# Scan branches that make the step sizes first, a third step-size tile loaded one unit sooner, and two images whose last projection reads its inputs from on-chip memory

## The chip, the cores and the metric

The kernel runs on one core of a Trainium2 chip. The metric is device time in microseconds (us) of the whole program, which works through a batch of eight images in one launch. The engines are called by the names of the profile: PE (TensorE, matrix products), DVE (VectorE), ACT (ScalarE), POOL (GpSimd) and SP (SyncE, which here does nothing but issue DMAs). Each engine takes its instructions in one fixed order, and an instruction that waits holds up everything behind it on its engine. That holds for SP too: a DMA that waits for its source, or for its target to come free, delays all DMAs that stand behind it.

## The reference

Four layers, each `x = x + layer(group_norm(x))`, on x of shape (8, 256, 32, 32) in float32. Layer 0 is an attention with eight heads of 64 whose q and k are normalised over the positions; layers 1 and 2 are 3x3 convolutions. Layer 3 is the long one; cut to what matters here, with N = 1024 positions and 256 channels in four groups of 64:

```python
def mamba(xs, inw, convw, convb, xpw, dtw, dtb, alog, dp, outw):   # one of 4 branches
    u, z = jnp.split(xs @ inw.T, 2, axis=-1)                       # 128 channels each
    u = silu(causal_conv4(u, convw) + convb)
    xdbc = u @ xpw.T
    dt = softplus(xdbc[..., :DTR] @ dtw.T + dtb)                   # step sizes
    Bm, Cm = xdbc[..., DTR:DTR + DS], xdbc[..., DTR + DS:]         # DS = 16 states
    # h[t] = exp(dt[t] * A) * h[t-1] + (dt[t] * u[t]) * Bm[t];  y[t] = sum_s h[t] * Cm[t]
    y = selective_scan(u, dt, Bm, Cm, -jnp.exp(alog), dp)          # ... + u * dp
    return y * silu(z) @ outw.T

xn = layernorm(xs); xm = mamba of the 4 groups + skip * xn; gates and 1-D convolutions -> xm2
x_local  = depthwise conv3 of xm2
x_global = mha(xm2)                                                # 8 heads of 32
x_out = concat([x_local, x_global]) @ fc_w.T + fc_b                # "the last projection" of the title
x_out = gelu(layernorm(x_out)); 2-D depthwise conv, layernorm, proj_w
```

## The kernel before

Per image there are three groups of work. The *front* is attention layer 0 and the two 3x3 convolutions (`front_attention`, `front_convs`). The *scans* are the four branches of the selective scan (`scan_layers`). The *back* is everything after them (`back_layers` with the second attention, `back_out` with the product by `fc_w`, `back_end`). The front and the back are dense and live on PE; the scans live on ACT, DVE and POOL. The outer loop runs over images b = 0..7, and in iteration b `interleave` mixes the dense stream (back of image b-1, front of image b+1) with the scans of image b: after every so many units of dense cost, one step of the scans is written out (`PACE`, 1.8 units for the first image, 2.78 for the middle six, 1.6 for the last). In iteration 0 there is no back, in iteration 7 no front, and after iteration 7 the back of image 7 runs alone. A scheduler then lays out each engine's order: by priority (the order in which the code writes the instructions), and by when it reckons that data and buffers are there. `Paced` keeps a scan instruction from standing ahead of the dense instructions that the code wrote before it on the same engine, so what the scheduler believes about a load's arrival decides how many dense instructions come between two scan instructions.

*One branch.* `branch_front` makes a branch's inputs in six steps, separated by `yield`: 0 the product into `raw`; 1 the convolution and silu into `u`; 2 `low`, the product that gives B and C, stored to DRAM as `bc` and read back broadcast; 3 the product for the step sizes into `a`, and the exponential for softplus; 4 the rest of softplus into `dt`, which `store` writes to DRAM (two DMAs `dt_m<-dt`); 5 `du = dt * u`, stored likewise (`du_m<-a`). `fronts` decides when the steps of branches 1 to 3 are done: in units of the scan, counted so that unit 0 of branch i has its first loads at 16 i, step 0 falls at 16 i - 17, and steps 1 to 5 at 16 i - 12, -10, -8, -6 and -3.

*The scan units.* `scan_steps` cuts a branch into 16 units: two halves of the positions (h), four groups of states (q), two pairs of channel groups (gp). One unit covers 128 partitions x 2 x 512. Its stages: `load` (three units ahead; du at the start of a half, B and C for every second unit), `load_dt` (one unit ahead, the dt tile at the start of a half, four DMAs of 128 KB), `drive` on POOL (two ahead, du * B into an `hs` tile, L974), `decays` on ACT (two exponentials `da<-dt,a_neg` into a PSUM tile), `scan` on DVE (two `hs<-da,hs`, or `hs<-da,carry,hs` in the second half), `weigh` on POOL (hs * C, L1006), and `add_up` on PE (`y<-hs,sel`), which at the end of a half lets DVE do `u<-u,half_d,y`. dt tiles come from pool `dtp` with two buffers, one for each gp; a new half's tile therefore takes the place of the tile that the old half used.

*Two small pools.* `wsp` holds weight chunks of 128 x 512 (six buffers); their loads are issued from ACT and wait there until the chunk's buffer is free. `hp` holds 128 x 512 tiles (two buffers) into which ACT copies the result of an attention pair, `both` or `rs`, which SP then stores to DRAM.

*The inputs of the last projection.* At the end of `back_layers` the four tiles (two `local`, two `o`) are written to a DRAM tensor `mix` (four DMAs of 512 KB, L1312), and `back_out` reads them back (L1379) into four new tiles before `project_both("fcw", ...)` multiplies them: 32 matrix instructions `big<-mix,w`. The attention tiles `o` are divided by their sums at the very end, by way of a small exchange over DRAM (`few<-sums`, `inv<-few_inv`, `rs<-inv`, then DVE `o<-o,rs`).

Of the kernel before, what the change touches and what calls it, by code (L numbers as in the profile page):

```python
# [19 lines left out]
P = 128  # L20
C = 256
N = 1024
# [11 lines left out]
def preact_stack(ctx: ExitStack, tc: tile.TileContext, I, out, cols):  # L34
# [7 lines left out]
    wp = ctx.enter_context(tc.tile_pool(name="wp", bufs=1))  # L42
    sp = ctx.enter_context(tc.tile_pool(name="sp", bufs=2))

    wsp = ctx.enter_context(tc.tile_pool(name="wsp", bufs=6))
    xp = ctx.enter_context(tc.tile_pool(name="xp", bufs=1))
    vp = ctx.enter_context(tc.tile_pool(name="vp", bufs=1))
    tp = ctx.enter_context(tc.tile_pool(name="tp", bufs=12))
    hp = ctx.enter_context(tc.tile_pool(name="hp", bufs=2))
    ps_big = ctx.enter_context(tc.tile_pool(name="ps_big", bufs=2, space=PSUM))  # L50
    ps_acc = ctx.enter_context(tc.tile_pool(name="ps_acc", bufs=1, space=PSUM))

# [11 lines left out]
    def work(name):  # L64
        return tp.tile([P, TP], F32, tag="t", name=name)
# [10 lines left out]
    def mwork(name):  # L76
        return mp.tile([P, N], F32, tag="m", name=name)
# [4 lines left out]
    def da_tile():  # L82
        return ps_da.tile([P, HALF], F32, tag="da", name="da")
# [730 lines left out]
    def store(br, name, src):  # L814

        br[name] = dp.tile([32, 2, 4, HALF], F32, tag=name, name=name + "_m")
        for h in range(2):
            nc.sync.dma_start(
                out=br[name][:, h].rearrange("d g n -> g d n"), in_=src[:, HALVES[h]]
            )  # L820

    def branch_front(i, xn, br):


        j, rows = i // 2, slice((i % 2) * 64, (i % 2) * 64 + 64)
        for h in range(2):
            ps = da_tile()
            tensor.matmul(
                ps,
                minw[rows, j, 0:P],  # L830
                inner(xn[j])[rows, HALVES[h]],
                start=True,
                stop=True,
            )
            scalar.copy(raw[:, 3 + h * HALF : 3 + (h + 1) * HALF], ps)
        yield
        u = mp.tile([P, N], F32, tag="u", name="u", bufs=2)
        uu = u[:, 0:N]
        scalar.activation(
            uu,  # L840
            raw[:, 3 : 3 + N],
            AF.Identity,
            bias=col("convb", i),
            scale=col("convw", 4 * i + 3),
        )
        for k in range(3):
            vector.scalar_tensor_tensor(
                uu, raw[:, k : k + N], col("convw", 4 * i + k), uu, ALU.mult, ALU.add
            )
        th = raw[:, 3 : 3 + N]  # L850
        scalar.activation(th, uu, AF.Tanh, scale=0.5)
        vector.scalar_tensor_tensor(uu, th, 1.0, uu, ALU.add, ALU.mult)
        br["u"] = u
        yield

        low = mwork("low")
        for h in range(2):
            ps = da_tile()
            tensor.matmul(
                ps[0 : 2 * DS], mxpw[:, i], u[:, HALVES[h]], start=True, stop=True  # L860
            )
            scalar.copy(low[0 : 2 * DS, HALVES[h]], ps[0 : 2 * DS])
        br["bc"] = dp.tile([DS, 2, 2, HALF], F32, tag="bc", name="bc")
        for k in range(2):
            nc.sync.dma_start(
                out=br["bc"][:, :, k],
                in_=low[k * DS : (k + 1) * DS].rearrange("s (h n) -> s h n", h=2),
            )
        yield

        a, dt = mwork("a"), mwork("dt")
        aa, ee, dd = a[:, 0:N], raw[:, 3 : 3 + N], dt[:, 0:N]
        for h in range(2):
            ps = da_tile()
            tensor.matmul(
                ps, mdtw[:, i], u[:, HALVES[h]], start=True, stop=True
            )
            vector.tensor_scalar_add(a[:, HALVES[h]], ps, col("dtb", i))  # L880
        scalar.activation(ee, aa, AF.Abs)
        scalar.activation(ee, ee, AF.Exp, scale=-1.0)
        yield
        vector.tensor_scalar_add(dd, ee, 1.0)
        vector.scalar_tensor_tensor(ee, dd, -1.0, ee, ALU.add, ALU.subtract)
        scalar.activation(dd, dd, AF.Ln)
        vector.tensor_sub(dd, dd, ee)
        vector.scalar_tensor_tensor(dd, aa, 0.0, dd, ALU.max, ALU.add)
        store(br, "dt", dd)
        yield  # L890
        vector.tensor_mul(aa, dd, uu)
        store(br, "du", aa)
        yield

    def branch_back(i, xn, br):
# [27 lines left out]
    def scan_steps(branches):  # L923
# [14 lines left out]
        def load_groups(u, name):  # L938
            br, g = branches[u["i"]], u["gp"] * 2
            if u["q"] == 0:  # L940
                t = dtp.tile([P, 2, HALF], F32, tag=name, name=name)
                src = br[name][:, u["h"], g : g + 2].rearrange("d g n -> d (g n)")
                for s in range(4):
                    nc.sync.dma_start(
                        out=t[s * 32 : s * 32 + 32].rearrange("d g n -> d (g n)"),
                        in_=src,
                    )
                br[name, u["gp"]] = t
            u[name] = br[name, u["gp"]]
# [80 lines left out]
        for n in range(-3, len(units) + 2):  # L1030
            done = None
            for ahead, stage in (
                (3, load), (1, load_dt), (0, decays), (0, None),
                (0, scan), (-1, weigh), (2, drive),
            ):
                if stage is None:
                    yield
                elif 0 <= n + ahead < len(units):
                    stage(units[n + ahead])
            if n % 2 and 0 <= n - 3 < len(units) - 1:  # L1040
                done = add_up(units[n - 3 : n - 1])
            yield done

    def scan_layers(img):


        xt = img.pop("x")
        img["stats"] = group_stats(img.pop("mv"), da_tile)
        xn = [xm_tile("xn0"), xm_tile("xn1")]
        for t in xn:  # L1050
            zero_ends(t)
        group_norm(tiles(xt), img["stats"], [inner(t) for t in xn])
        img["xd"] = xdp.tile([P, 2, N], F32, tag="xd", name="xd")
        nc.sync.dma_start(out=img["xd"], in_=xt)
        sq = [mwork("ln_sq"), mwork("ln_sq")]
        yield
        yield from layer_norm(
            [inner(t) for t in xn], sq, BY_HALF, da_tile, affine("norm_w", "norm_b")
        )
        yield  # L1060
        branches = [{} for _ in range(NB)]
        for _ in branch_front(0, xn, branches[0]):
            yield

        def fronts():
            for i in range(1, NB):
                for n, _ in enumerate(branch_front(i, xn, branches[i])):
                    yield 16 * i - 12 + 9 * n // 4

        front, ending, due, n = fronts(), iter(()), 0, 0  # L1070
        steps = scan_steps(branches)
        while True:
            next(ending, None)
            while due is not None and n >= due:
                due = next(front, None)
            if next(steps, END) is END:
                break
            yield
            done = next(steps)
            if done is not None:  # L1080
                ending = branch_back(done, xn, branches[done])
            n += 1
            yield
        yield from ending
        img["xm"] = xn
# [123 lines left out]
    def back_layers(img, exact=False):  # L1209
# [82 lines left out]
        yield from project("fpw", fd, evac_x2)  # L1292


        img["mix"] = xdp.tile([4, P, N], F32, tag="mix", name="mix")
        local = []

        def add_local():
# [9 lines left out]
                next(img["begin"])  # L1308
        while len(local) < 2:
            add_local()  # L1310
        for t, part in enumerate(local + img.pop("o3")):
            nc.sync.dma_start(out=img["mix"][t], in_=part[:, 0:N])  # L1312

    def merge_weights():

# [58 lines left out]

    def back_out(img):

        srcs = [work("mix")[:, 0:N] for _ in range(4)]
        for t in range(4):
            nc.sync.dma_start(out=srcs[t], in_=img["mix"][t])  # L1379
        yield 0  # L1380
        xo = img["xo"] = [work("xo")[:, 0:N] for _ in range(2)]

        def evac_fc(m, ps):
            scalar.activation(xo[m], ps, AF.Identity, bias=fc_b[:, m : m + 1])

        yield from project_both("fcw", srcs, evac_fc)
# [124 lines left out]
    PLACES = [1, 4, 4, 4, 4, 5, 6, 8, 9, 10, 11, 12, 13, 14, 15, 16]  # L1511
    PLACES += [18, 20, 22, 24, 26, 27, 28, 29]
    EARLY = 3
    PACE = [1.8] + [2.78] * (batch - 2) + [1.6]
    imgs = [{} for _ in range(batch)]
    drain(
        amid(front_attention(image_of(0), imgs[0]), merge_weights(), (8,)),
        front_convs(imgs[0]),
# [51 lines left out]
    again = nc.values_load(flag[0:1, 0:1], min_val=0, max_val=1)  # L1570
    with tc.If(again > 0):
        with tc.For_i(0, batch, 1) as i:
            img = {}
            src = x_in[bass.ds(i, 1)].rearrange("o (t p) n -> p (o t) n", p=P)
            dst = out[bass.ds(i, 1)].rearrange("o c n -> (o c) n")
            drain(front_attention(src, img, True), front_convs(img), scan_layers(img))
            drain(back_layers(img, True), back_out(img), back_end(img, dst))
# [109 lines left out]
```

## Time and profile before

| | us |
|---|---|
| median of 3 runs | 6550.79 (6543.21 to 6555.45) |
| the profiled execution | 6534.17 |
| its span | 6532.5 |
| PE busy | 5503.0 (84% of the span) |
| DVE / ACT / POOL busy | 4003.1 / 2701.2 / 2737.3 |
| iteration 0 (from the store of image 0's `xd` to that of image 1's) | 375.0 to 1028.6 |
| iterations 1 to 6, each | 776.5, 765.3, 769.6, 761.2, 761.2, 761.3 |
| iteration 7, until DVE's scans end | 5623.7 to 6209 |
| the back of image 7, after that | to 6532.5 |

How to read the profile. Most instructions pass through one helper (L105), so they are told apart by the tiles they write and read: `da<-dt,a_neg` is the decay, `hs<-du,bc` is the drive. A row of the groups has count, then busy us, mean ns of one, then the engine's idle time just before such instructions and what ended it. In the timeline a number in square brackets is idle time of the engine before the entry. `SPq` is SP issuing a DMA. "issue" in the chain of waits is time in which the engine waited for nothing that the profile can name.

### The profile page before, as it was taken

Reading aid. Unit: us, or ns where it says so; the run is one execution under the profiler, and the core shown is the slowest. Engines: PE = TensorE matmul, PEld = TensorE weight load, DVE = VectorE, ACT = ScalarE, POOL = GpSimd, SP = SyncE. Lnnn points to the kernel's source line nnn. Section 1 sums busy time; section 2 is a strip of 40 time slices with the busy share of each in tenths; the row PEclk is TensorE's granted clock in tenths of the full one; section 3 lists DMA queues with packets and bytes.
Section 4 is the critical chain, followed back from the end, with each engine's and each line's share of the span. In section 5 each row is a group of like instructions: output and inputs, shape, how many; then the busy total and the mean of one; then the engine's idle time right before and its main releaser. Section 6 shows DMA issues by size and latency. Waiting matters only on the chain.

```text
span 6532.5 us, 52259 instructions
## 1 busy us (share of the span) xinstructions
PE 5503.0 (84%) x17318; PEld 1846.7 (28%) x17318; DVE 4003.1 (61%) x4613; ACT 2701.2 (41%) x3241; POOL 2737.3 (42%) x1302
## 2 busy tenths in 40 slices
PE   8886688899888988989889898899889898876496
PEld 2331133223332233222332233322332223311222
DVE  5247845577556775567756776567855777555622
ACT  3223424644255532644236442555326442344242
POOL 0006653634435353543517345263435435276500
PEclk9997889999899989999899998999899998988697
DMA  1022232323233132321223222231323212233301
GB/s 44 26 62 76 78 89 76 88 74 88 69 91 98 39 93 77 101 85 57 81 82 99 75 75 80 83 103 44 91 77 101 87 57 82 77 82 88 97 26 43
DMA packets 224761, 495.99 MB, mean 76 GB/s; under 512 B 61016, under 2 KB 102616, under 8 KB 223456
## 3 DMA queue, kind: packets, MB, share of 16 engines
q1 hardware_dynamic: 168032, 419.12, 22.2%
q10 hardware_dynamic: 56448, 73.43, 3.9%
q8 instruction: 139, 2.28, 0.1%
q14 instruction: 142, 1.16, 0.1%
HBM read 411.09 MB, written 72.88 MB: 74 GB/s over the span
## 4 chain that ended last, share of the span: by engine, by line
PE 53%; DVE 24%; issue 6%; DMA 6%; ACT 6%; POOL 4%; SPq 1%; ACTq 0%; DVEq 0%; POOLq 0%
PE big L105 33%; PE acc L105 11%; DVE hs L105 6%; PE da L105 5%; DVE p L105 4%; DVE dw L105 3%; POOL hs L1006 3%; PE y L105 3%; DVE u L105 2%; DVE t L105 1%; DMA du_m<-a 1%; POOL hs L974 1%; ACT p L105 1%; ACT da L105 1%; DMA dt<-dt_m 1%
## 5 line engine op out<-in xcount | busy, mean ns | idle before, releaser
L974 POOL TENSOR_TENSOR hs<-du,bc 128x1024 f32<-128x1024 f32 x512 | 1339.7, 2636 | 1623.2 <-DMA du<-du_m 683.0
L1006 POOL TENSOR_TENSOR hs<-hs,bc 128x1024 f32<-128x1024 f32 x512 | 1303.7, 2547 | 1027.7 <-DVE hs L105 841.2
L105 ACT ACTIVATE p<-big 128x1024 f32<-128x1024 f32 x1024 | 1038.5, 1021 | 735.0 <-PE big L105 724.2
L105 PE MATMUL acc<-p,v 128*64 128x512 f32 x4096 | 1151.8, 636 | 8.8 <-ACT both L105 6.0
L105 ACT ACTIVATE da<-dt,a_neg 128x512 f32<-128x512 f32 x1024 | 684.2, 686 | 1144.7 <-DVE hs L105 442.1
L105 PE MATMUL big<-im,w 128*128 128x512 f32 x2304 | 1104.0, 631 | 20.4 <-ACT im L105 20.4
L105 DVE TENSOR_TENSOR p<-p 128x1024 f32<-128x1024 f32 x448 | 720.0, 1607 | 295.2 <-ACT p L105 201.8
L105 DVE TENSOR_TENSOR_SCAN hs<-da,carry,hs 128x512 f32<-128x512 f32 x512 | 623.5, 1265 | 256.4 <-ACT da L105 176.0
L105 DVE TENSOR_TENSOR_SCAN hs<-da,hs 128x512 f32<-128x512 f32 x512 | 599.7, 1209 | 286.6 <-ACT da L105 267.6
L105 PE MATMUL big<-qk,qk 64*128 64x512 f32 x2048 | 647.9, 663 | 95.2 <-ACT p L105 85.5
L105 PE MATMUL y<-hs,sel 128*32 128x512 f32 x2048 | 454.0, 674 | 315.3 <-POOL hs L1006 314.8
L105 PE MATMUL big<-q,k 64*128 64x512 f32 x2048 | 616.8, 660 | 107.2 <-ACT p L105 60.6
L105 PEld LDWEIGHTS big<-im,w 128*128 128x128 f32 x2304 | 446.9, 201 | 689.5 <-issue 642.1
L1005 POOL COPY carry<-hs 128x2 f32<-128x2 f32 x256 | 104.2, 407 | 823.0 <-DVE hs L105 745.0
L105 PEld LDWEIGHTS acc<-p,v 128*64 128x64 f32 x4096 | 213.7, 137 | 820.3 <-issue 719.0
L105 PEld LDWEIGHTS big<-qk,qk 64*128 64x128 f32 x2048 | 178.2, 192 | 537.1 <-issue 280.1
L105 PEld LDWEIGHTS big<-q,k 64*128 64x128 f32 x2048 | 165.8, 190 | 535.5 <-issue 252.6
L105 DVE SCALAR_TENSOR_TENSOR dw<-xo,vec,dw 128x961 f32<-128x961 f32 (+1 forms) x128 | 247.8, 1972 | 16.4 <-ACT dw L105 15.2
L105 PEld LDWEIGHTS y<-hs,sel 128*32 128x32 f32 x2048 | 58.6, 112 | 616.7 <-POOL hs L1006 456.4
L105 PE MATMUL big<-xn,w 128*128 128x512 f32 x512 | 230.1, 601 | 0.0
L105 DVE SCALAR_TENSOR_TENSOR u<-raw,vec,u 128x1024 f32<-128x1024 f32 x96 | 136.2, 1419 | 87.1 <-ACT u L105 85.3
L105 PE MATMUL big<-w,xn 128*128 128x512 f32 x256 | 137.2, 687 | 42.6 <-ACT big L105 34.9
(214 smaller groups left out, 5085.5 us busy)
## 6 DMA issues: line engine op xcount, KB each, us to landing
bc<-bc SPq DMA_DIRECT2D x1024, 128.0 KB
du<-du_m SPq DMA_DIRECT2D x512, 128.0 KB
dt<-dt_m SPq DMA_DIRECT2D x512, 128.0 KB
w<-in_wc ACTq DMA_DIRECT2D x192, 192.0 KB
rs<-inv SPq DMA_DIRECT2D x64, 256.0 KB
dt_m<-dt SPq DMA_DIRECT2D x64, 256.0 KB
du_m<-a SPq DMA_DIRECT2D x64, 256.0 KB
mix<-mix SPq DMA_DIRECT2D x32, 512.0 KB
```

The source lines that it names most:

```text
L105: made = issue(*args, **kwargs)
L974: nc.gpsimd.tensor_mul(u["hs"], u["du"], both_groups(u["bc"][:, 0]))
L1005: nc.gpsimd.tensor_copy(carry[:, u["q"], g : g + 2], hs[:, :, HALF - 1])
L1006: nc.gpsimd.tensor_mul(hs, hs, both_groups(u["bc"][:, 1]))
```

## The change

1. `branch_front`: the step that makes `low` (B and C) moves from third to last, behind dt and du. `fronts` takes the times from a tuple, so that the steps (now raw, u, a, dt, du, low) fall at 16 i - 18, -12, -10, -8, -7, -6. (A step is made when the count reaches the time that the step before it gave.)
2. dt tiles have three buffers in place of two, and `load_dt` runs two units ahead in place of one.
3. To make room, `wsp` goes from six to five buffers and `hp` from two to one.
4. For the last two images (`direct`), and in the fallback that does not run, `mix` is not written to DRAM: `back_out` multiplies the four tiles where they lie.

```diff
-    wsp = ctx.enter_context(tc.tile_pool(name="wsp", bufs=6))
+    wsp = ctx.enter_context(tc.tile_pool(name="wsp", bufs=5))
...
-    hp = ctx.enter_context(tc.tile_pool(name="hp", bufs=2))
+    hp = ctx.enter_context(tc.tile_pool(name="hp", bufs=1))
...
         br["u"] = u
         yield
-        low = mwork("low")
-        for h in range(2):
-            ps = da_tile()
-            tensor.matmul(
-                ps[0 : 2 * DS], mxpw[:, i], u[:, HALVES[h]], start=True, stop=True
-            )
-            scalar.copy(low[0 : 2 * DS, HALVES[h]], ps[0 : 2 * DS])
-        br["bc"] = dp.tile([DS, 2, 2, HALF], F32, tag="bc", name="bc")
-        for k in range(2):
-            nc.sync.dma_start(
...
-        yield
...
         vector.tensor_mul(aa, dd, uu)
         store(br, "du", aa)
         yield
+        low = mwork("low")
+        for h in range(2):
...
+        yield
...
-                t = dtp.tile([P, 2, HALF], F32, tag=name, name=name)
+                bufs = 3 if name == "dt" else 2
+                t = dtp.tile([P, 2, HALF], F32, tag=name, name=name, bufs=bufs)
...
-                (3, load), (1, load_dt), (0, decays), (0, None),
+                (3, load), (2, load_dt), (0, decays), (0, None),
...
-                for n, _ in enumerate(branch_front(i, xn, branches[i])):
-                    yield 16 * i - 12 + 9 * n // 4
+                for at, _ in zip(FRONT, branch_front(i, xn, branches[i])):
+                    yield 16 * i + at
...
-        for t, part in enumerate(local + img.pop("o3")):
-            nc.sync.dma_start(out=img["mix"][t], in_=part[:, 0:N])
+        parts = [t[:, 0:N] for t in local + img.pop("o3")]
+        if img.get("direct"):
+            img["mix"] = parts
+            return
+        for t, part in enumerate(parts):
+            nc.sync.dma_start(out=img["mix"][t], in_=part)
...
-        srcs = [work("mix")[:, 0:N] for _ in range(4)]
-        for t in range(4):
-            nc.sync.dma_start(out=srcs[t], in_=img["mix"][t])
+        srcs = img["mix"]
+        if not img.get("direct"):
+            srcs = [work("mix")[:, 0:N] for _ in range(4)]
+            for t in range(4):
+                nc.sync.dma_start(out=srcs[t], in_=img["mix"][t])
...
+    FRONT = (-12, -10, -8, -7, -6, -2)
...
-    imgs = [{} for _ in range(batch)]
+    imgs = [{"direct": b >= batch - 2} for b in range(batch)]
...
-            img = {}
+            img = {"direct": True}
```

## The prediction

> **What bounds the kernel now.** I read the page's engine shares first, then a table of busy time by stage, because the iterations have different limits: iteration 0, one of the six alike in the middle, iteration 7, and the back of image 7 alone.
>
> ```profile
> PE 5503.0 (84%) x17318; PEld 1846.7 (28%) x17318; DVE 4003.1 (61%) x4613; ACT 2701.2 (41%) x3241; POOL 2737.3 (42%) x1302
> ...
> 375.00:1028.60 653.60, 486.63 (x1372) 151.51 (x1373) 416.52 (x458) 232.39 (x300) 350.17 (x160) 0.86 0.27 76
> 4862.40:5623.70 761.30, 670.57 (x2160) 225.88 (x2160) 505.98 (x573) 336.95 (x406) 343.91 (x160) 0.94 0.28 81
> 5623.70:6190.00 566.30, 363.15 (x1116) 115.38 (x1116) 319.52 (x331) 223.24 (x275) 302.69 (x151) 0.77 0.31 87
> 6190.00:6533.00 343.00, 259.57 (x852) 94.75 (x850) 97.64 (x141) 115.07 (x116) 22.02 (x10) 0.86 0.11 36
> ```
>
> The columns are PE, weight loads, DVE, ACT, POOL, the granted PE clock, and the DMAs' share and GB/s. A middle iteration is PE's: 671 of 761 us busy, 91 us idle. Iteration 7 is nobody's: PE 363 of 566, POOL 303, so it is made of waits. Who waits for whom, over the whole span:
>
> ```profile
> POOL hs L1006 <- DVE hs L105: 841.2, 160, 21.9
> ...
> DVE hs L105 <- ACT da L105: 443.5, 162, 15.0
> ...
> PE y L105 <- POOL hs L1006: 314.8, 114, 19.7
> ...
> ACT da L105 <- DMA dt<-dt_m: 276.0, 26, 26.6
> ```
>
> Read upwards: the decays wait for dt tiles, DVE's scan for the decays, POOL for the scan, PE's sum for POOL. The timeline shows how such a wait arises, where the second half of branch 1 begins in image 7 (SP, DVE, then ACT):
>
> ```profile
> 5859.17 1.23 SPq L959 DMA_DIRECT2D bc<-bc  x3
> 5882.84 1.18 SPq L818 DMA_DIRECT2D dt_m<-dt  x2
> 5884.07 0.49 SPq L959 DMA_DIRECT2D bc<-bc  x1
> 5884.67 8.53 SPq L944 DMA_DIRECT2D dt<-dt_m  x8
> ...
> 5880.94 0.75 DVE L105 SCALAR_TENSOR_TENSOR u<-u,half_d,y 128x512 f32<-128x512 f32 x1 [9.83 <-PE y L105]
> 5881.60 1.22 DVE L105 SCALAR_TENSOR_TENSOR dt<-a,dt 128x1024 f32<-128x1024 f32 x1
> ...
> 5896.59 3.63 DVE L105 TENSOR_TENSOR_SCAN hs<-da,carry,hs 128x512 f32<-128x512 f32 x3 [10.24 <-ACT da L105]
> ...
> 5894.49 1.28 ACT L105 ACT_TABLE_LOAD   x1 [23.85 <-DMA sums<-both]
> ```
>
> SP stands 22 us at `dt_m<-dt`, the store of branch 2's step sizes, because DVE makes dt only behind `u<-u,half_d,y`, which waits for the end of the first half. The loads of the second half's own dt stand behind that store; ACT idles 23.85 us (put down to `sums<-both`, but what follows is a decay, and its dt landed just then). From DVE's timeline, the pauses in the scans at the seven changes of half are 12, 1, 20, 20, 15, 31, 26 us in image 0 (125 in all) and 12, 19, 27, 19, 23, 16, 12 in image 7 (128). Last, the two waits for `mix`, each ahead of 32 products:
>
> ```profile
> 6061.50 8.64 PE L105 MATMUL big<-mix,w 128*128 128x512 f32 x16 [29.60 <-DMA mix<-mix]
> ...
> 6430.01 15.58 PE L105 MATMUL big<-mix,w 128*128 128x512 f32 x32 [13.11 <-issue]
> ```
>
> **What the Trainium skill says.** "DMA: Bandwidth & Descriptors", section "Anatomy of one DMA", says that DMA engines do not wait on semaphores: a wait is taken on the issuing sequencer before dispatch. The 22 us at the store agree, with loads behind it that needed nothing from it. "Perfetto Trace Analysis", section "Optimization Strategy", says that the same gap repeating can mean too few buffers for the next tile; the pauses at every half agree in kind, for the dt tile has one buffer per channel pair. "TensorE: Matmul & The Clock Gate", section "HAM oscillation", says that idle gaps of PE over about 3.4 us lead to a throttled clock; the table agrees in direction (0.77 in iteration 7, 0.94 in the middle), so a gap removed is worth a little more than its length. I put no number on this.
>
> **The change part by part.** Neither the number of engine instructions nor their shapes change; 16 DMAs of 512 KB go. Everything is a matter of order and waits, so I compare the order of instructions on each engine in the two built programs, which holds no times.
>
> *Direct inputs, image 7.* PE waits 13.1 us at 6416.9, then needs 15.6 us, to 6445.6. Three of four tiles are ready long before; the fourth, `o`, is finished by DVE at 6429.5 (timeline). Directly, 24 products (24 x 0.49 = 12 us) run from 6416.9 to 6429, the other 8 (4 us) to 6433.5. Gain 12 us, all on the path; what is late next is the exchange of the sums, unchanged.
>
> *Direct inputs, image 6.* PE stands 29.6 us from 6031.9; `o` is ready at 6059.9. Likewise 24 products move into the wait and the rest end near 6064 in place of 6078. The sums `y` that stand among these products hold up POOL and DVE. Gain 14 us for the scans behind it, counted in image 7 below.
>
> *Step sizes first, third tile, sooner load.* In the built order dt's last DVE step stood, in units of image 7's scan, at 7.5, 24.0 and 40.0 for branches 1 to 3; a half ends at 8, 24 and 40. After the change it stands at 6.5, 22.5, 38.5, du half a unit later. So the store no longer waits for the end of the half, and the dt loads behind it follow. From dt to the first decay: du 1.2 us, four stores of 0.6, three loads of 0.45, and some 4.5 us to land (the chain of waits has 4.35 and 4.47 for such loads), about 9; against it run the three scans still to do (3.8 us). A pause of 5 us is left of 12, 27 and 23. Where a branch begins (19, 19, 16), ACT's order had 11, 10 and 4 dense instructions between the last decay and the next; after, 5, 6 and 0: 15 fewer at about 1 us. The third tile allows this: the load need not wait for the old half's last decay. The `low` step, now last, is 2 products, 2 copies of 0.57 us and two stores; its loads are for a half that begins six units later, 25 us at POOL's pace, so I cost it at nothing; if it came late, POOL would wait as it does for du today.
>
> POOL gives part back: its 325 us (302.7 + 22.0 in the table) for 64 units are some 40 us a half back to back, and the halves of 27 to 37 us in image 7 lived off what POOL did in the pauses. Pause and scans of the three second halves (12 + 30, 27 + 27, 23 + 46) go from 42 to 40, from 54 to 42, and from 69 to 44 (with image 6's 14 us in it); of the 15 at branch starts I take 8. Image 7: 2 + 12 + 25 + 8 = 47 us.
>
> *Image 0.* ACT's dense instructions at the changes go from 34 to 19. PE's waits there (timeline: 10.9 and 6.8 at 549 to 579, 5.2 and 6.3 at 681 to 706) are 29 us; PE is 74% busy, I take 25.
>
> *Images 1 to 6.* Only what PE waits counts. In iteration 6, from PE's timeline: 9.7 + 2.6 us while image 6's first dt is made and loaded; 6.4 at 5131 where branch 1's second half begins; 21.6 us in waits over 2.5 us for `y` during the convolutions. Of the first I take 2.5 (`low`'s two products and copies no longer stand ahead of dt, but the 10 us landing of `du_m` stays), of the second all 6, of the third 5, since DVE is full there. That is 13.5, say 13, x 6 = 78 us. Its bounds are 0 (PE fills up elsewhere) and 25.
>
> *Fewer small buffers.* One `hp` tile: a copy must wait until the stores of the copy before have landed. In the middle images the copies are at least 16.5 us apart, their stores issue within 7.4 us and land about 2 later: 0 us. In image 7 one copy at 6005 would have waited 15.6 us (the stores before it were issued 44 us late, behind the dt store that now comes earlier): 0 to 16, I take 0. Behind that copy on ACT stand decays and exponentials. Five weight chunks: a convolution uses one per 5.3 us (12 products; 144 in 63.9 us), so four ahead is 21 us against a load of a few us: 0. But each issue waits on ACT for a chunk to come free (in all 727 us of idle ahead of the `in_wc` loads, ACT's timeline), with decays behind it. The new order places each a chunk later, so I take 0; if it did not, up to 24 x 5.3 = 127 us of ACT waiting per image.
>
> **Sum.** 12 + 47 + 25 + 78 = 162 us off the profiled span of 6532.5 (execution 6534.2), so 6370. The median of the runs lies 17 us above the profiled execution: 6551 - 162 = 6389.
>
> **Rivals.** *Ends only (0.22).* PE's 91 idle us in the middle are spread over many waits, most of them not for scans, and the order merely shifts them. Then 12 + 40 + 15 = 67: 6484. For it speaks that DVE, not ACT, is full during the convolutions; against it the 6 us that hang on one dt load. *More than counted (0.06).* The `y` waits go wholly and PE's clock rises: 25 x 6 + 75 + 12 + 30, 6285. *Slower (0.11).* The weight ring: ACT's issues wait a chunk longer, and a third of 127 us per image reaches PE through late decays: 42 x 6 = 250 less the 162 gained, about 6640. It decides from 27 us per middle image on. For it speaks the 727 us that already wait there; against it that the loads stand later in ACT's order. *No change (0.03).* The gains and the ring cancel. That the load isn't sooner after all is ruled out by SP's order: a half's first four dt loads now stand ahead of the four `bc` loads that preceded them.
>
> **Numbers.** Likeliest (0.58): 6389. Its own bounds: 0 and 25 per middle image, 25 to 70 for image 7, 10 to 40 for image 0, hence 47 to 272 less; joined with the first rival and the outer half of the others, 6290 to 6515. About 0.2% (13 us) is what a measurement can tell from no change. Faster 0.86, within 0.03, slower 0.11.
>
> **What would show it.** Right: ACT's wait for `dt<-dt_m` falls from 276 us to under 150; image 7's pauses from 128 to near 60; PE's wait ahead of image 7's last products vanishes; a middle iteration takes 745 to 752 us. Wrong: the middle stays at 761 (ends only), or ACT's idle time ahead of `in_wc` loads grows and the convolutions stretch (the ring).

## The result and the profile after

The changed kernel took 6562.67 us (median of 11 runs, 6555.16 to 6572.76), the kernel before, beside it on the same chip, 6549.64 (11 runs). The ratio is 1.0022, 95% interval 1.0011 to 1.0033: slower by a little where 2.5% less was forecast. The profiled execution has a span of 6560.4 us against 6532.5. First the engines' busy times (from the page), then the stages, cut at the same events as before: iteration 0, iteration 6, iteration 7 until DVE's last scan, and the back of image 7. The columns are length, PE, weight loads, DVE, ACT, POOL, granted PE clock, DMA share and GB/s.

```profile
PE 5504.5 (84%) x17318; PEld 1847.3 (28%) x17318; DVE 3978.8 (61%) x4613; ACT 2704.2 (41%) x3241; POOL 2722.8 (42%) x1302
...
373.90:1034.40 660.50, 489.14 (x1372) 153.17 (x1373) 420.91 (x457) 232.10 (x300) 345.52 (x160) 0.84 0.27 75
4899.80:5678.00 778.20, 674.46 (x2160) 227.85 (x2160) 501.29 (x573) 337.85 (x406) 341.57 (x160) 0.93 0.28 79
5678.00:6251.50 573.50, 389.08 (x1156) 117.91 (x1156) 337.63 (x347) 231.40 (x285) 321.99 (x159) 0.77 0.30 82
6251.50:6560.40 308.90, 242.77 (x812) 88.85 (x810) 80.85 (x125) 107.34 (x106) 3.04 (x2) 0.88 0.07 21
```

The work is the same, instruction for instruction. The end became shorter, the middle longer (us, from the same marks; the last column is the fifth experiment, all of the change except the fronts' order and places):

| stage | before | after | fronts put back |
|---|---|---|---|
| iteration 0 | 653.6 | 660.5 | 644.3 |
| iteration 1 | 776.5 | 762.4 | 744.9 |
| iterations 2 to 6 together | 3818.6 | 3881.2 | 3798.1 |
| iteration 7, to the last scan | 585.2 | 573.5 | 575.4 |
| back of image 7 | 323.6 | 308.9 | 307.9 |

The four waits that carried the forecast, of the changed kernel:

```profile
POOL hs L1007 <- DVE hs L105: 873.8, 147, 21.8
DVE hs L105 <- ACT da L105: 414.2, 152, 18.4
PE y L105 <- POOL hs L1007: 291.3, 108, 7.5
ACT da L105 <- DMA dt<-dt_m: 142.1, 22, 27.2
```

ACT's wait for dt fell from 276.0 to 142.1 us, as forecast ("under 150"), and the pauses at the half changes of image 7 from 129 to 49. Both signs came true and the time did not follow. DVE's timeline says why: the eight halves of image 7 between those pauses took 363.5 us before and 440.0 after. 80 us of pause went, 76 came back inside the halves. In branch 1, for example, first half, pause and second half were 56 + 27 + 27 and became 76 + 6 + 33.

Where a half grows is seen where branch 2 of image 5 changes its half. First the timelines of SP. The half's last scan ends at 4630.1 before and at 4662.0 after. Before:

```profile
4628.98 1.18 SPq L818 DMA_DIRECT2D dt_m<-dt  x2
4630.20 5.92 SPq L944 DMA_DIRECT2D dt<-dt_m  x6
4639.30 4.76 SPq L959 DMA_DIRECT2D bc<-bc  x4
4644.16 1.07 SPq L818 DMA_DIRECT2D du_m<-a  x2
```

After:

```profile
4517.83 0.31 SPq L945 DMA_DIRECT2D dt<-dt_m  x1
4518.68 0.34 SPq L523 DMA_DIRECT2D inv<-few_inv  x1
4519.06 0.89 SPq L945 DMA_DIRECT2D dt<-dt_m  x2
4520.35 1.09 SPq L530 DMA_DIRECT2D rs<-inv  x2
4521.49 0.58 SPq L945 DMA_DIRECT2D dt<-dt_m  x1
...
4647.73 1.20 SPq L818 DMA_DIRECT2D dt_m<-dt  x2
4651.02 1.11 SPq L818 DMA_DIRECT2D du_m<-a  x2
4652.17 2.84 SPq L960 DMA_DIRECT2D bc<-bc  x2
4660.06 1.28 SPq L889 DMA_DIRECT2D bc<-low  x2
4661.38 3.94 SPq L945 DMA_DIRECT2D dt<-dt_m  x4
```

The next half has two dt tiles of four loads each. Before, the last two loads of its first tile stand right behind dt's store, 0.1 and 0.7 us after the end of the old half. In the changed kernel the third buffer has let the whole first tile be loaded 140 us ahead of that end (`dt<-dt_m` at 4517.8 to 4521.5), so the four loads at 4661.4 are those of the second tile. By the order of the three buffers theirs was free at 4649.6, when the last decay on the tile that held it ended, and dt is stored 14.3 us ahead of the end of the half instead of 1.1; but the stores of du and low stand between, and the loads are issued 12 us after their buffer was free. SP takes its entries in order, and stands from 4655 to 4660 at `bc<-low`, because low isn't made yet. "Perfetto Trace Analysis", section "DMA Instruction — HWDGE (DVE, Sync)", says that the start the profiler reports is the moment when the waits are over; so SP's wait is the gap ahead of an entry, not its length, and the gap agrees. The other engines at the same place (ACT, DVE, PE):

```profile
4648.87 0.69 ACT L105 ACTIVATE da<-dt,a_neg 128x512 f32<-128x512 f32 x1 [0.60 <-DVE hs L105]
...
4658.23 0.57 ACT L105 COPY low<-da 32x512 f32<-32x512 f32 x1 [8.67 <-PE da L105]
4658.84 0.69 ACT L105 ACTIVATE da<-dt,a_neg 128x512 f32<-128x512 f32 x1
...
4662.11 12.16 ACTq L159 DMA_DIRECT2D w<-in_wc  x2
4674.47 0.69 ACT L105 ACTIVATE da<-dt,a_neg 128x512 f32<-128x512 f32 x1 [11.73 <-PE big L105]
...
4650.91 2.32 DVE L105 TENSOR_TENSOR_SCAN hs<-da,hs 128x512 f32<-128x512 f32 x2
4659.63 2.39 DVE L105 TENSOR_TENSOR_SCAN hs<-da,hs 128x512 f32<-128x512 f32 x2 [6.39 <-ACT da L105]
...
4653.51 1.62 PE L105 MATMUL y<-hs,sel 128*32 128x512 f32 x4 [4.78 <-POOL hs L1007]
4655.06 2.08 PE L105 MATMUL big<-im,w 128*128 128x512 f32 x2
4657.07 1.98 PE L105 MATMUL da<-u,w_mxpw 128*32 128x512 f32 x4
```

Read from below: PE waits 4.8 us for POOL before it sums y; behind that stand low's products; ACT waits 8.7 us for them, with the decays of the half's last units behind its copy; DVE then lacks decays for 6.4 us; and SP holds the dt loads behind low's store. The 6.4 us are most of what this half is longer (115.0 us, 106.4 before). The held loads did not even end a wait here: they had landed by 4667.9, and the decays on their tile start at 4674.5, behind the second of two loads of weights, which ACT issues at 4673.9.

### The profile page after: what moved, and what is told of

It reads as the page before. It is cut to its first block, busy times and chain, and to the rows that moved or that the text cites. A ratio compares the mean times of both kernels' runs of the same rounds, so it can differ in the third digit from the quotient of the medians.

```text
span 6560.4 us, 52297 instructions
## 1 busy us (share of the span) xinstructions
PE 5504.5 (84%) x17318; PEld 1847.3 (28%) x17318; DVE 3978.8 (61%) x4613; ACT 2704.2 (41%) x3241; POOL 2722.8 (42%) x1302
## 4 chain that ended last, share of the span: by engine, by line
PE 52%; DVE 24%; ACT 7%; issue 6%; DMA 6%; POOL 5%; SPq 1%; ACTq 0%; DVEq 0%; POOLq 0%
PE big L105 34%; PE acc L105 11%; DVE hs L105 7%; PE da L105 5%; DVE p L105 3%; PE y L105 3%; POOL hs L1007 3%; POOL hs L975 2%; DVE dw L105 2%; DVE t L105 2%; DVE u L105 2%; DMA du_m<-a 1%; ACT p L105 1%; ACT da L105 1%; DMA dt<-dt_m 1%
## 5 line engine op out<-in xcount | busy, mean ns | idle before, releaser
L975 POOL TENSOR_TENSOR hs<-du,bc 128x1024 f32<-128x1024 f32 x512 | 1308.8, 2575 | 1701.4 <-DMA du<-du_m 1209.6
L105 PE MATMUL big<-im,w 128*128 128x512 f32 x2304 | 1133.2, 644 | 75.3 <-ACT im L105 71.3
L105 DVE TENSOR_TENSOR p<-p 128x1024 f32<-128x1024 f32 x448 | 695.1, 1552 | 309.8 <-ACT p L105 216.3
L1006 POOL COPY carry<-hs 128x2 f32<-128x2 f32 x256 | 126.8, 495 | 874.5 <-DVE hs L105 795.7
L105 PE MATMUL da<-xn,w_minw 64*128 64x512 f32 x256 | 161.1, 740 | 52.3 <-DVE hs L105 49.6
```

What stands on the lines that cost most here:

```text
L105: made = issue(*args, **kwargs)
L975: nc.gpsimd.tensor_mul(u["hs"], u["du"], both_groups(u["bc"][:, 0]))
L1006: nc.gpsimd.tensor_copy(carry[:, u["q"], g : g + 2], hs[:, :, HALF - 1])
```

## The experiments

My first reading was another one. In the changed kernel PE waits longer ahead of the second convolution of the middle images (from the end of the first convolution to the start of the second 27.3 us in place of 15.8), because scans and other DVE work now stand between the small operations of its group norm. The first four runs were to test this *norm theory* by taking the parts apart. All ratios are against runs of the kernel before on the same chip, with 95% intervals; differences between runs of different rounds are taken from the ratios, times 6547 us (the median of before).

**1 to 4: parts alone.** The first keeps only the direct inputs of the last two images (`imgs = [{"direct": b >= batch - 2} ...]` and what uses it). The second has only the fronts:

```diff
         br["u"] = u
         yield
-        low = mwork("low")
...
         store(br, "du", aa)
         yield
+        low = mwork("low")
...
-                    yield 16 * i - 12 + 9 * n // 4
+                    yield 16 * i + at
...
+    FRONT = (-12, -10, -8, -7, -6, -2)
```

The third has only the third tile, its sooner load and the small pools:

```diff
-    wsp = ctx.enter_context(tc.tile_pool(name="wsp", bufs=6))
+    wsp = ctx.enter_context(tc.tile_pool(name="wsp", bufs=5))
...
-    hp = ctx.enter_context(tc.tile_pool(name="hp", bufs=2))
+    hp = ctx.enter_context(tc.tile_pool(name="hp", bufs=1))
...
+                bufs = 3 if name == "dt" else 2
...
-                (3, load), (1, load_dt), (0, decays), (0, None),
+                (3, load), (2, load_dt), (0, decays), (0, None),
```

The fourth joins the first two. Expected:

> Only the last two images keep the inputs of the last projection on the chip; all else as in the kernel before (step (a) of the prediction and the share of step (b) that is image 6's). Norm theory (the changed kernel loses its time in iterations 2 to 6, where scans stand between the small operations of the group norm ahead of the second convolution): iterations 2 to 6 as before within 2 us each, iteration 7 and the tail together 12 to 26 shorter, time 12 to 26 us below before. Weight-ring theory (the loss comes from five weight slots instead of six): the same, since six slots are kept. Theory that the direct inputs themselves cost something (four tiles held longer): time at or above before.

> Only the order of the fronts: step sizes first, low and its transfers last, with the new list of places. Two dt tiles, loaded one unit ahead, six weight slots, all images through HBM. Norm theory: no scan stands inside the chain ahead of the second convolution of the middle images (g to shift stays at 6 to 7 us), so no iteration is longer than before by over 3 us; the pauses at the first dt shrink, and the time is 0 to 40 us below before. Theory that the fronts' order is the cause (later low and bc, so the scans' B and C come late): iterations 2 to 6 are longer by 8 to 15 each, time 40 to 70 above before.

> Only the third dt tile, loaded two units ahead, and the small pools that pay for it (five weight slots, one hp buffer); fronts in the old order, all images through HBM. Norm theory: scans and other work stand inside the chain ahead of the second convolution of the middle images (8 of them by the order of DVE's instructions), g to shift takes 13 to 20 us instead of 6.3, iterations 2 to 6 are 5 to 12 longer each, and the time is 20 to 60 above before. Theory that the fronts' order is the cause: iterations at or below those of before, time 0 to 60 below.

> The fronts' new order and the direct inputs, without the third tile, the sooner load and the smaller pools. Norm theory: the gains of the two parts add, 15 to 60 us below before, the fastest kernel so far. Theory that the fronts' order is the cause: above before by 20 to 50.

| run | median us | ratio | interval |
|---|---|---|---|
| direct inputs alone | 6519.3 | 0.9964 | 0.9953 to 0.9975 |
| fronts alone | 6576.9 | 1.0049 | 1.0031 to 1.0066 |
| third tile, sooner load, small pools | 6450.3 | 0.9857 | 0.9836 to 0.9878 |
| fronts and direct inputs | 6545.6 | 1.0004 | 0.9992 to 1.0015 |

The norm theory fell at once (run 3 was to be 20 to 60 us slower by it). The other one, that the fronts' order costs, had the signs of runs 2 and 3 and missed the sizes: run 2 is 35 us above before where 40 to 70 was expected, run 3 is 91 below where up to 60 was, and run 4 is level where 20 to 50 more was expected. With the third tile alone the time from one convolution to the next is nearly that of the changed kernel (26.4 us), and PE's idle time ahead of `big<-im,w` is up from 20.4 to 94.5 us over the span, yet this kernel is 1.4% faster than before. The second convolution is 12 us shorter (111 us for 124, image 5), since four of the 60 sums y that stood in it go earlier. The wait was real, but the time in it came back in the second convolution. The fronts are what costs.

**5 to 8: which part of the fronts.** The fifth is the changed kernel with the fronts of before. The sixth moves low later, by `FRONT = (-12, -10, -8, -7, -3, -1)`; its last number also puts raw at 16 i - 17 again. The seventh is the fifth with `yield 16 * i + FRONT[n]` and the changed kernel's numbers. The eighth is the kernel before with the two small pools only.

> The changed kernel with the fronts put back: old order (low third), old places; third tile, sooner load, small pools and direct inputs stay. If the fronts alone lose what the other parts bring, the gains of the third tile (91 us) and of the direct inputs (22 us) nearly add: 100 to 115 below before, 6425 to 6445, middle iterations at 755 to 760, the first convolution of the middle images at 106 us as in the run with the third tile alone (118 in the changed kernel). If the parts shared one gain: no better than 6450.

> The changed kernel with the one number moved that places low: FRONT is (-12, -10, -8, -7, -3, -1), so that low falls at 16 i - 3 in place of 16 i - 6, and a, dt and du stay early. Theory L (low, made where a half changes, puts its two products behind PE's wait for y and its two copies ahead of the decays of the half's last units): DVE no longer waits for decays early in the first convolution, which shrinks from 118 to about 106 us, iterations 2 to 6 lose about 10 each, time 6450 to 6510. Theory D (dt and du, made inside the half, take DVE's time from the half's last scans): no iteration changes by over 3 us, time 6545 to 6575.

> The changed kernel with low third again (steps raw, u, low, a, dt, du) at the new places: low at 16 i - 10, a at -8, dt at -7, du at -6. Theory L: low is away from the change of half, the first convolution is at 106 us, time 6430 to 6470. Theory D: dt is a unit later than in the changed kernel and a unit sooner than in the kernel before, du three units sooner than before, so some of the loss stays: first convolution 108 to 115 us, time 6480 to 6550.

> The kernel before with five weight slots and one hp buffer, nothing else. The prediction's rival (the weight ring holds ACT, decays come late): slower, by up to 100 us, with ACT's idle time ahead of the in_wc loads above 727 us. Costed at nothing by the prediction: within 10 us of before, stage by stage.

| run | median us | ratio | interval |
|---|---|---|---|
| all but the fronts | 6446.6 | 0.9846 | 0.9826 to 0.9867 |
| changed, low late | 6518.1 | 0.9958 | 0.9943 to 0.9972 |
| all but the fronts, old order at the new places | 6572.5 | 1.0039 | 1.0028 to 1.0051 |
| small pools alone | 6545.5 | 1.0004 | 0.9991 to 1.0016 |

Without the fronts' part the change is worth 1.5%. So the fronts cost 115 us (1.0022 less 0.9846), over three times what they cost alone (32): they take back the whole gain of the third tile. The scans in the traces say where. Each sum is over the 24 halves in which the next branch's front is made (the first halves of branches 0 to 2): their length from the first scan of the second unit to the last scan, and the change of half behind them, from that last scan to the first scan of the next half's second unit.

| us | before | changed | fronts put back (run 5) | low late (run 6) |
|---|---|---|---|---|
| the 24 halves | 1494.9 | 1579.1 | 1489.1 | 1476.4 |
| the 24 changes of half | 428.7 | 335.0 | 345.1 | 387.9 |

So the fronts cost 90 us in these halves and nothing at the changes of half, where the dt loads are; 41 stand at the starts of branches, and all else sums to -16. Moving low (with raw) takes 103 us out of the halves, though dt and du stay early: low, made inside the half, is what lengthened them. Runs 2, 4 and 14, which also make low at 16 i - 6, have 1562.7, 1554.8 and 1604.2 there, and no other run has over 1533.8. But 53 come back at the changes, so that run 6 wins back 42 of the 115; its 6518.1 lies above what theory L allowed (6510) and below theory D (6545). The first convolution (image 5) shrank only from 118.6 to 114.1, not to 106, though the decays in question no longer wait for low. That the old order at the new places takes 6572.5, more than either theory allowed, left neither L nor D whole. The small pools alone cost nothing: the weight-ring rival of the prediction is out for the kernel before. (Beside the third tile six weight chunks were not tried.)

**9 to 12: one place at a time.** Base is the fifth run, 6446.6. As the list that each step's successor waits for (so u falls at the first number, raw at the last less 16), its places in the old order are (-12, -10, -8, -6, -3, -1). Changed to (-12, -10, -8, -6, -6, -1) for du, (-12, -10, -8, -7, -3, -1) for dt, (-12, -10, -8, -6, -3, -2) for raw. The twelfth is the changed kernel with `FRONT = (-12, -8, -6, -3, -2, -1)`.

> Third tile, direct inputs and the old order of the fronts, at the old places except du, which moves from 16 i - 3 to 16 i - 6, in the same count as dt. Base: the run with the third tile and direct inputs, 6446.6. Theory S (du ahead of the half's dt loads: SP takes du's two stores between dt's store and those loads, and DVE does du ahead of the scans that are still to come, so each half change comes later): 40 to 110 above the base. Theory R (raw a unit sooner is what costs): within 15 of the base.

> Third tile, direct inputs, old order, old places except dt, which moves from 16 i - 6 to 16 i - 7. My prediction's step (dt out of the half's end lets its loads follow sooner): 0 to 30 below the base of 6446.6. Theory D (dt's four DVE operations, put ahead of the half's last scans, lengthen the half by as much as the pause shrinks, and more): 0 to 60 above.

> Third tile, direct inputs, old order, old places except raw, which moves from 16 i - 17 to 16 i - 18. Theory R: the product for raw and its copies fall among the scans of the branch before and cost 40 or more above the base of 6446.6. Theories S and D: within 10 of it.

> The changed kernel with the new order of steps (low last) at late places: raw at 16 i - 17, u at -12, a at -8, dt at -6, du at -3, which are the old ones, and low at -2 in place of -10. If the places alone cost (theories S, D, R): within 20 of the base of 6446.6. If low after dt and du costs wherever it stands (its store and its bc loads then fall just ahead of the new branch's start): 30 to 80 above.

| run | median us | ratio | interval | against the base |
|---|---|---|---|---|
| du early | 6512.6 | 0.9950 | 0.9933 to 0.9967 | +68 |
| dt early | 6471.1 | 0.9880 | 0.9860 to 0.9899 | +22 |
| raw early | 6459.9 | 0.9864 | 0.9843 to 0.9885 | +12 |
| new order, late places | 6461.1 | 0.9871 | 0.9851 to 0.9891 | +16 |

The three places sum to 102 of the 126 that they cost together (run 7). du is the largest, and the only one whose interval stands clear of the base's. dt made a unit earlier (the change makes it two units earlier) at any rate won nothing: run 10 has the sign of theory D, and run 11 lies between its two forecasts. The new order as such, at late places, costs little or nothing.

**13 and 14: SP's queue or the operations.** When du moves, its multiplication moves on DVE and its two stores on SP. The thirteenth separates them:

```diff
         store(br, "dt", dd)
-        yield
         vector.tensor_mul(aa, dd, uu)
+        yield
         store(br, "du", aa)
         yield
```

The fourteenth is the changed kernel with du computed at -7 and low at -6 as there, but both stores in a step of their own, `FRONT = (-12, -10, -8, -7, -6, -3, -2)`.

> The third tile with direct inputs and the old fronts (6446.6), with du's multiplication in dt's step at 16 i - 6, as in the run with du early (6512.6), but du's two stores at 16 i - 3, where they were. Theory S (SP's queue: du's stores ahead of the dt loads): the dt loads follow dt's store at once again, time within 15 of 6447. Theory D (DVE's multiplication ahead of the scans): within 15 of 6513.

> The changed kernel with every computing step where it was (a at 16 i - 10, dt at -8, du at -7, low at -6) but the stores of du and of low in one step at -3, behind the next half's first dt loads on SP. Theory S: the dt loads come sooner than in any run so far, and the time is 6430 to 6480. Theory D: within 20 of the changed kernel's 6563. Between them: the share of the 116 us that SP's order makes.

The thirteenth took 6447.1 us (0.9852, 0.9829 to 0.9874), the base's time: du's multiplication costs nothing there, the place of its two stores 64 us (0.9950 less 0.9852). Nothing else differs much between runs 9 and 13: the order of the instructions on ACT, DVE and POOL is the same in their traces but for 10, 13 and 11 of them, moved by at most three places. The same half change as above, in SP's timeline, with du's stores early (run 9; the half ends at 4614.2):

```profile
4613.12 1.19 SPq L818 DMA_DIRECT2D dt_m<-dt  x2
4616.41 1.11 SPq L818 DMA_DIRECT2D du_m<-a  x2
4617.56 2.74 SPq L945 DMA_DIRECT2D dt<-dt_m  x2
```

and late (run 13; the half ends at 4578.1):

```profile
4577.02 1.18 SPq L818 DMA_DIRECT2D dt_m<-dt  x2
4578.25 1.48 SPq L945 DMA_DIRECT2D dt<-dt_m  x2
4579.83 5.58 SPq L960 DMA_DIRECT2D bc<-bc  x4
4586.84 1.09 SPq L818 DMA_DIRECT2D du_m<-a  x2
```

The loads (the last two of the next half's second tile) issue 4.4 us after dt's store, or 1.2. The means over the 24 changes of half behind a front, in us from the last scan of the old half:

| | second tile's last load issued | landed | first unit's first scan | second unit's first scan |
|---|---|---|---|---|
| before | 9.1 | 14.1 | 11.3 | 17.9 |
| changed | 3.5 | 7.1 | 7.6 | 14.0 |
| fronts put back (run 5) | 3.8 | 9.5 | 7.8 | 14.4 |
| du early (run 9) | 7.8 | 14.1 | 7.0 | 17.6 |
| its multiplication alone early (run 13) | 3.6 | 9.3 | 8.1 | 14.3 |

The first unit is not late in run 9: with the third buffer its tile is loaded 48 us ahead of that last scan. The second unit is, by 3.3 us, 80 over the 24 changes, of which 22 are made up in the halves behind them; its decays start within 1 us of the landing of their tile in 22 of the 24, in run 13 in 8. In the changed kernel, by contrast, the second tile's loads come no later than with the fronts put back (3.5 and 3.8): there the stores of du and low use up what an earlier dt could have brought, and its 115 us go elsewhere, as the sums above show. The waits of run 9 and of run 13 agree:

```profile
DVE hs L105 <- ACT da L105: 500.3, 156, 16.2
ACT da L105 <- DMA dt<-dt_m: 229.7, 35, 25.6
```

```profile
DVE hs L105 <- ACT da L105: 404.9, 147, 16.2
ACT da L105 <- DMA dt<-dt_m: 121.7, 21, 22.2
```

The fourteenth took 6497.5 us (0.9936, 0.9915 to 0.9958), between the two theories and 56 less than the changed kernel. It does not part the stores from the computing steps: the step of their own is also a seventh step of branch 0's front, and 1392 of ACT's 3161 instructions (table loads left out) and 1858 of DVE's 4613 stand at other places in their order than in the changed kernel. The second tile's last load is now issued 1.6 us ahead of the end of the half, but the 24 halves stay long (1604.2). So of the 115 us the place of low, with raw's, is 42 by run 6, and how the rest divides among dt, du, the stores and the starts of branches is not shown. (dt a unit early and raw early, alone, were 22 and 12, neither clear of the base.)

A kernel that beats both is thus the change without its fronts: 0.9846 of the time before, the lowest ratio of all (run 13 and the third tile alone are equal to it within the intervals). The direct inputs, worth 24 us alone, show only 7 beside the third tile, less than the intervals can tell.

## Why the prediction was wrong

- *Direct inputs, image 7's tail: 12 us.* Right. From the last scan to the end it was 323.6 us; with the direct inputs alone 311.1, in the changed kernel 308.9. PE goes through the `local` products and the first eight of `o` where it waited 13.1 us before:

```profile
6459.61 7.13 PE L105 MATMUL big<-local,w 128*128 128x512 f32 x16
6466.58 3.60 PE L105 MATMUL big<-o,w 128*128 128x512 f32 x8
6472.70 5.40 PE L105 MATMUL big<-o,w 128*128 128x512 f32 x8 [2.52 <-DMA x_in<-xd]
```

- *Image 7's scans: 47 us.* The stage gained 12 (585.2 to 573.5). The pauses went as forecast; the term that failed is the length of the halves, for which I allowed 40, 42 and 44 us of pause and second half (41, 38 and 59 came) and looked at no first half. Those of branches 1 and 2 went from 56 and 53 to 76 and 67.5. Even with the fronts put back the halves of image 7 sum to 422.8 us in place of 363.5, so the pauses there were worth little in any case.
- *Image 0: 25 us.* The iteration became 7 longer; with the fronts put back 9 shorter.
- *Images 1 to 6: 78 us.* Iterations 1 to 6 became 48 longer (4595.1 to 4643.6). This is the step that decided, and two terms of it failed. `low`, "now last", was cost "at nothing": made inside the half, it puts its copies, which wait for PE, ahead of the half's last decays, and the 24 halves grew by 90 us against the fronts put back (run 6, with low late, takes 103 away). And "So the store no longer waits for the end of the half, and the dt loads behind it follow" had the wrong loads and left out a wait: with the third tile the first tile's loads are on average 47 us ahead of that end without the new fronts (run 5), and those of the second tile stand behind du's stores, which I priced at 0.6 us each behind 1.2 of du, though du's store comes 3.3 us after dt's at the place shown. Runs 9 and 13 price that place alone at 64 us. In the changed kernel an earlier dt therefore brought these loads forward by 0.4 us on average. With the fronts put back iterations 1 to 6 are 52 us shorter (4543.0; 4539.6 with the third tile alone). The bound of 0 per middle image ("PE fills up elsewhere") excluded a loss without a reason.
- *Third tile, small pools.* The third tile and the sooner load did what the step said: ACT's wait for dt fell to 159.5 us with them alone, and the kernel to 0.9857, 94 us of the 162 forecast for the whole. Small pools at 0 was right by run 8, and nothing is left of the ring rival's 250 us.
- *The rivals.* None was the outcome. "Ends only" is nearest in kind, but the middle did not stay, it lost, and by another mechanism than the one rival that I gave on that side. A rival "the moved steps hold the scans and the loads" belonged there: I had named SP's 22 us stand at a store as the trouble of the kernel before, and the change puts the stores of du and low ahead of dt loads.

## What to carry to other kernels

A step that issues DMAs from an in-order queue is moved with its waits: ask what each moved store waits for, and put it behind the loads that someone is about to need; two stores of 0.6 us in the wrong place cost 1% in one experiment, and deferring only the stores, not the arithmetic, gave all of it back. A small step put into a stretch that is already full can cost more than its instructions: ask what stands behind it on each engine. Two parts of a change that aim at the same wait are to be measured apart: here a third buffer had already taken away the wait that the reordering was made for. A pause that closes is not time gained until the stretches beside it have been measured too. A new wait on the bound engine is a suspect, not a cause: undo one part at a time before believing it.

## What was not expected of the hardware

- "DMA: Bandwidth & Descriptors", section "Issuing engines are not separate DMA queues", calls the sequencer's time to initiate a DMA usually small beside the DMA. The 0.6 us per store agree: a store of dt landed 7.5 us after its issue (median, kernel before). What costs is the wait ahead of it, in which nothing else of that queue is issued: 5.1 us ahead of low's store in the lines above (4655.0 to 4660.1), 2.1 ahead of du's (4648.9 to 4651.0).
- Loads right behind a store also land late. In the trace of the kernel before, a dt load issued within 6 us after a store of dt or du landed after 7.8 us (median of 96), any other after 2.75 (416). Of the sixteen marks of such a landing twelve come first and the last four 4.5 us later (median); that the store holds them is not tested. Between runs 9 and 13 this is the smaller part: the second tile lands 4.8 us later, and 4.2 of them are later issue.
- PE's busy time in the middle is not fixed by its instructions. Between the first convolutions of images 2 and 7, some 10,800 products, it was per image 674.6 us before, 677.8 with the direct inputs alone, where the same instructions run (its profiled execution was the longest of its ten), and 668.8 with all but the fronts; PE's idle time in these was 89.0, 90.7 and 89.6. So what the fastest kernel gains there shows as busy time of PE, 5.8 us per image, where two programs that are alike there differ by 3.2, one execution each. The granted clock of the stretch is 0.93 in all three. Why is open.
